# The spectral unit's residual: products with a flipping matrix, or an add on VectorE

## The chip, the cores and the metric

The kernel runs on one core of a Trainium2 chip. The metric is the device time of one execution in microseconds (us). All data is fp32.

## What is computed

The reference is a two-layer block on x of shape (8, 128, 32, 32): 8 images, 128 channels, 1024 tokens each. Every step adds to its own input:

```python
x = x + attention(ln_c(x))          # layer 0, first half
t = to_tokens(x)                    # (8, 1024, 128)
t = t + spectral(ln_t(t))           # layer 0, second half (the STU)
x = from_tokens(t)
x = x + deformable_conv(ln_c(x))    # layer 1, first half
t = to_tokens(x)
t = t + experts(ln_t(t))            # layer 1, second half: 8 experts, the best 2
```

The change concerns one plus sign: the `t +` ahead of the spectral part. That part is a causal convolution over the tokens with 16 filters at four resolutions, each followed by a 128x128 mixing matrix, and three lagged products.

## The kernel before, in words

**Stages.** Attention for all 8 images comes first and writes its result, with its own residual added, to a DRAM tensor `x1d` of shape (image, 128, 8, 128). Then one long stage does the spectral part of all images and, laid between its products, the second layer of the image before. The second layer of the last image runs alone at the end.

**Token orders.** In `x1d[b]` row p holds 8 groups of 128 channels: group par * 4 + i is token 2 * (128 * i + p) + par, so even tokens stand in the first four groups and odd ones in the last four. The spectral part works on tokens in reversed order: an indirect load on POOL's queue (in `prepare`, L1391) reads the rows of `x1d[b]` from the last to the first into a tile `x1`. The norm's source for images 2 to 7 is this tile; for images 0 and 1 the normalised tokens come from loads of their own, made during attention.

**The spectral loop** (`spectral_and_second_layer`). Its work list is (image, filter), 8 x 16 periods, in program order, written out by hand: each engine takes its instructions in that order. A period has two halves (src 0 and 1, the even and odd source tokens). In each half `filter_image` makes three PSUM banks, named p_x, p_y and p_z (L1488). ScalarE turns p_x out twice (L1499, L1500), POOL adds the two (L1501), VectorE takes p_y (L1506, L1509) and p_z (L1516) out with further adds. The sums `us` are mixed one or two periods later: `mix` (L1453, through `add`) multiplies them with the mixing matrices `mf` and accumulates in `po`, a pair of PSUM banks with one buffer for the whole image. The filters of three periods ahead are loaded on SP (L1257, L1258; three buffers, so that the load waits for the products of the present period), and the matrices two periods ahead (L1357; for the first image they are made on VectorE, L1379 and L1381).

**The residual in it.** Ahead of the first mixing product of an image, `start_sums` multiplies each of the 8 groups of `x1` (as weights) with `flip`, the 128x128 matrix with ones on the other diagonal. The product is a turned and re-reversed group, so `po` begins with the residual, in (channel, token) layout, and all other products add to it. The first matmul in each of the two banks carries the start flag (`add` keeps the list `opened`). After the last filter, `finish` copies `po` to `x2` (channels by tokens), one half by ScalarE (L1529) and the other by VectorE (L1530).

**The second layer.** `points` starts with `turn_back`: four TensorE transposes for each half of `x2` into a bank p_back (L1168), and a ScalarE copy of each bank (L1169) to `tok` (128 tokens by 8 groups by channels; group a, row q is token 128 * a + q). Then come the norm of `tok` on VectorE (statistics at L788 and L789), its turn (p_turn, L919), products, the writing of a table to DRAM, and the sampling positions. `sampled` gathers rows of that table (POOL's queue), weighs and sums them on ScalarE and VectorE, takes a norm, and runs the experts (p_e, L1123; L1135, L1140, L1143 on VectorE). Both are generators. `advance` runs them a step at a time in the slots between the spectral products, by a time budget: RATE 3.2 us a slot, and each step says how much it takes. Right after `finish` the new `second_layer(b)` is put at the head of its row, so that `turn_back` is issued in that slot. Apart from `po`, all of the spectral stage's and second layer's PSUM tiles come from one pool of six banks, taken in turn. After the last image, `layer.image` and what is left of the image before alternate, a step each.

Of the kernel before, what the change touches and what calls it, by code (L numbers as in the profile page):

```python
# [11 lines left out]
F32 = mybir.dt.float32  # L12
I32 = mybir.dt.int32
AF = mybir.ActivationFunctionType
ALU = mybir.AluOpType
# [3 lines left out]
P = 128  # L19
B = 8  # L20
C = 128
T = 1024
NT = T // P
HT = T // 2
# [3 lines left out]
NF = 16  # L28
# [774 lines left out]
class DeformAndExperts:  # L803
# [2 lines left out]
    ROWS = T + 33  # L806

    def __init__(
        self, ctx, tc, ident, dram, conv_w, conv_b, off_w, off_b, mask_w, mask_b,
        router_w, router_b, expert_w, expert_b, out, banks,  # L810
    ):
        self.nc = tc.nc
        self.cp = ctx.enter_context(tc.tile_pool(name="d_const", bufs=1))
        self.sb = ctx.enter_context(tc.tile_pool(name="d_sb", bufs=2))
        self.ps = ctx.enter_context(tc.tile_pool(name="d_ps", bufs=banks, space=PSUM))
        self.ident, self.dram, self.out = ident, dram, out
        self.given = (
            conv_w, conv_b, off_w, off_b, mask_w, mask_b, router_w, router_b, expert_w, expert_b
        )
# [162 lines left out]
        got.extend((idx, w))  # L982
        yield

    def image(self, b, x2):

        got = []
        yield from self.points(b, x2, got, True)
        yield from self.sampled(b, got, True)

    def points(self, b, x2, got, alone):


        nc, sb = self.nc, self.sb
        newton = nc.vector if alone else nc.gpsimd
        tok = sb.tile([P, NT, C], F32, tag="tok", name="tok")
        yield from self.turn_back(x2, tok)
        yield
        ht = sb.tile([P, NT, C], F32, tag="ht", name="ht")
        yield from norm_steps(nc, sb, tok, ht, 1e-6, newton, not alone)  # L1000
        yield 1.0 if alone else 5.0
        hc = sb.tile([C, T], F32, tag="hc", name="hc")
        yield from self.turn_steps(ht, hc)
        nc.gpsimd.tensor_tensor(tok, tok, self.cb.unsqueeze(1).to_broadcast([P, NT, C]), ALU.add)
        yield


        tab = self.tabs[b % 2]
        N = TAPS * C + TAPS * 9
        gs = sb.tile([P, NT, N], F32, tag="gs", name="gs", bufs=1)  # L1010
        writes = []

        def write():
            if writes:
                i0, tap, slot, back = writes.pop(0)
                r0 = 33 - back + i0 * P
                queue = nc.scalar if alone and slot % 2 else nc.sync
                queue.dma_start(
                    tab[tap, r0 : r0 + 4 * P, slot, :].rearrange("(i p) c -> p i c", p=P),
                    gs[:, i0 : i0 + 4, tap * C : (tap + 1) * C],  # L1020
                )

        for i in range(NT):
            pg = self.bank("p_g")
            nc.tensor.matmul(
                pg[:, 0:N], hc[:, i * P : (i + 1) * P], self.gw, start=True, stop=True
            )
            nc.scalar.copy(gs[:, i, :], pg[:, 0:N])
            if i % 4 == 3:
                writes += [  # L1030
                    (i - 3, tap, slot, back)
                    for tap in range(TAPS) for slot, back in enumerate((0, 1, 32, 33))
                ]
            for _ in range(4 if alone else 2):
                write()
            yield 1.0 if alone else 1.5
        while writes:
            for _ in range(4 if alone else 2):
                write()
            yield 1.0 if alone else 1.7  # L1040
        po = self.bank("p_om")
        for tap in range(TAPS):
            at = TAPS * C + 9 * tap
            nc.tensor.matmul(
                po[:, 0 : 9 * NT], self.shift[tap], gs[:, :, at : at + 9],
                start=(tap == 0), stop=(tap == TAPS - 1),
            )
        om = sb.tile([P, NT, 9], F32, tag="om", name="om")
        nc.vector.tensor_tensor(
            om, po[:, 0 : 9 * NT].rearrange("p (i k) -> p i k", k=9), self.base, ALU.add  # L1050
        )
        yield
        yield from self.corners(om, got)
        got.append(tok)
# [104 lines left out]
                yield  # L1159
        nc.sync.dma_start(self.out[b].rearrange("c h w -> c (h w)"), ot)  # L1160

    def turn_back(self, src, dst):

        for half in range(2):
            pt = self.bank("p_back")
            for i in range(4):
                t0 = (half * 4 + i) * P
                self.nc.tensor.transpose(pt[:, i * P : (i + 1) * P], src[:, t0 : t0 + P], self.ident)  # L1168
            self.nc.scalar.copy(  # L1169
                dst[:, half * 4 : half * 4 + 4, :].rearrange("p a c -> p (a c)"), pt  # L1170
            )
            yield

    def gates(self, tt, got, wait):
# [122 lines left out]
class Spectral:  # L1297
# [88 lines left out]
    def prepare(self, b):  # L1386

        nc, sb = self.nc, self.sb
        img = {"b": b, "ur": self.given.ur[b % 2], "gap": self.given.given.gap[b % 2]}
        img["x1"] = sb.tile([P, NT, C], F32, tag="x1", name="x1", bufs=2)  # L1390
        nc.gpsimd.indirect_dma_start(  # L1391
            out=img["x1"].rearrange("p i c -> p (i c)"), out_offset=None,
            in_=self.x1d.rearrange("b p i c -> (b p) (i c)"),
            in_offset=bass.IndirectOffsetOnAxis(ap=self.back[:, b : b + 1], axis=0),
        )

        img["ut"] = sb.tile([C, 3, HT + 1], F32, tag="ut", name="ut")
        return img
# [30 lines left out]

    def start_sums(self, img):  # L1430

        po = img["po"] = self.op.tile([P, 2, 2, HT // 2], F32, tag="o", name="po")
        img["opened"] = set()
        for par in range(2):
            for i in range(4):
                out = po[:, i // 2, par, (i % 2) * P : (i % 2 + 1) * P]
                self.add(img, i // 2, out, img["x1"][:, par * 4 + i, :], self.flip)

    def add_lags(self, img):

# [92 lines left out]
def spectral_and_second_layer(tc, spec, layer, weights):  # L1533
    work = [(b, k) for b in range(B) for k in range(NF)]
    imgs = {0: spec.prepare(0)}
# [10 lines left out]
    rows = [deque([spec.channels(imgs[0], layer.bank), layer.setup()]), deque()]  # L1546
    starts = {}
    todo = [0.0, 0.0]

    def second_layer(b):  # L1550
        got = []
        yield from layer.points(b, imgs[b]["x2"], got, False)
        rows[1].append(layer.sampled(b, got, False))

    def advance(time):
# [34 lines left out]
    for n in range(len(work) + 2):  # L1590
        now = work[n] if n < len(work) else None
        if now is not None:
            b, k = now
            if k == 1 and b + 1 < B:
                starts[b + 1] = spec.begin(b + 1, layer.bank, imgs)
                rows[0].append(starts[b + 1])
            elif k == 0 and b:
                for _ in starts[b]:
                    pass
            us = sums[n] = spec.sb.tile([C, 2, 2, HT], F32, tag="us", name="us", bufs=3)  # L1600
        for src in range(2):
            run = iter(())
            if now is not None:
                run = spec.filter_image(imgs[b], src, filters[n], less[n], us, layer.bank)
            for slot, spans in enumerate((SPANS[0:3], SPANS[3:4])):
                next(run, None)
                m = n - 2 + src
                if 0 <= m < len(work):
                    img, k = imgs[work[m][0]], work[m][1]
                    if src == 1 and slot == 0 and k == 0:  # L1610
                        spec.start_sums(img)
                    if src == 1 and slot == 0 and k == 1:
                        spec.add_lags(img)
                    spec.mix(img, 1 - src, spans, mf[m], sums[m], k == NF - 1)
                    if src == 0 and slot == 1 and k == NF - 1:
                        spec.finish(img)
                        if img["b"] + 1 < B:
                            rows[0].appendleft(second_layer(img["b"]))
                if now is not None:
                    advance(RATE if b + 1 < B else LAST_RATE)  # L1620
            next(run, None)
            if now is not None:
                between(n, src)
        if n + 3 < len(work):
            filters[n + 3] = spec.load_filter(work[n + 3][1])
        if NF <= n + 2 < len(work):
            mf[n + 2] = spec.read_matrices(work[n + 2][1])

    runs = [layer.image(B - 1, imgs[B - 1]["x2"]), chain(*rows[0], *rows[1])]
    while runs:  # L1630
        runs = [r for r in runs if next(r, r) is not r]

# [2 lines left out]
def metaformer_kernel(  # L1635
# [30 lines left out]
    with branch.Else():  # L1666
# [4 lines left out]

    spec = Spectral(ctx, tc, dram, phi_e, phi_o, M_u, M_plus, M_minus, coef, x1d, back, begin)
    layer = DeformAndExperts(
        ctx, tc, ident, dram, conv_w, conv_b, off_w, off_b, mask_w, mask_b,
        router_w, router_b, expert_w, expert_b, out, 6,
    )
    with tc.manual_schedule(engines=None):
# [51 lines left out]
```

## Time and profile before

| what | value |
|---|---|
| median of 3 runs | 2700.72 us (2695.61 to 2702.18) |
| the profiled execution | 2699.79 us |
| its span, first to last instruction | 2698.0 us |
| mean granted TensorE clock | 0.974 |
| busy: TensorE matmul | 2530.0 us, 94% of the span |
| busy: TensorE weight load (overlaps the matmuls) | 1769.3 us, 66% |
| busy: VectorE | 1852.9 us, 69% |
| busy: ScalarE | 1083.5 us, 40% |
| busy: GpSimd (POOL) | 1448.6 us, 54% |
| moved by DMA | 267.10 MB, 99 GB/s over the span |

Attention takes the first 910 us or so, the spectral stage with the second layer of images 0 to 6 runs to about 2560 us, and the last image's second layer to the end. The names in the profile leave buffer numbers out: `x1`, `x2` and `x3` all read `x`, so `po<-flip,x` is the product of `start_sums`, `x<-po` the copies of `finish`, and `p_back<-ident,x` the transposes of `turn_back`. PE is TensorE's matmul, PEld its weight load, DVE VectorE, ACT ScalarE, SPq the queue of SP. An fp32 product appears as two weight loads and two matmuls.

### The profile page before, as it was taken

What the parts mean: (1) busy time and instruction counts of PE and PEld (TensorE: products, weight loads), DVE (VectorE), ACT (ScalarE), POOL (GpSimd) and SP (SyncE); (2) the same over time, 40 slices, a digit from 0 to 9 for tenths busy, and PEclk for the clock granted to TensorE, in tenths of its full rate; (3) what the DMA queues carried; (4) which work ended last, traced back from release to release, by engine and by line L of the source; (5) the groups of instructions that cost most, each with busy time, mean ns of one, the idle gap of its engine ahead of it and who ended that gap; (6) DMA issues with size and microseconds to landing.
All of it is one profiled execution on the core that took longest, in us unless ns stands there. A gap on an engine that the chain in (4) does not pass through costs nothing. (4 is left out here: it accounts for less than half of the span.)

```text
span 2698.0 us, 47432 instructions
## 1 busy us (share of the span) xinstructions
PE 2530.0 (94%) x18896; PEld 1769.3 (66%) x18896; DVE 1852.9 (69%) x2728; ACT 1083.5 (40%) x2030; POOL 1448.6 (54%) x1535
## 2 busy tenths in 40 slices
PE   6999999999999799999999999999999999999924
PEld 3555555555555578777787787778778778777712
DVE  3888888888888455448648649648648657658646
ACT  4666766667667111123223224224214224224232
POOL 4777777777788455446246237237236227226230
PEclk9999999999999899999999999999999999999956
DMA  1000000000000254375275266265266266256151
GB/s 29 2 17 2 17 17 2 17 9 10 9 17 17 83 162 153 119 207 160 73 212 169 71 198 184 71 191 176 79 181 194 71 173 194 79 149 202 40 168 35
DMA packets 204675, 267.10 MB, mean 99 GB/s; under 512 B 20308, under 2 KB 138260, under 8 KB 204448
## 3 DMA queue, kind: packets, MB, share of 16 engines
q1 hardware_dynamic: 181312, 205.27, 26.1%
q0 software_dynamic: 16800, 55.59, 6.2%
q10 hardware_dynamic: 6336, 3.15, 0.4%
q8 instruction: 151, 2.47, 0.4%
q14 instruction: 76, 0.62, 0.1%
HBM read 196.02 MB, written 67.92 MB: 98 GB/s over the span
## 5 line engine op out<-in xcount | busy, mean ns | idle before, releaser
L623 POOL TENSOR_TENSOR t<-e 128x1024 f32<-128x1024 f32 x256 | 608.3, 2376 | 199.3 <-ACT e L614 199.0
L651 DVE TENSOR_TENSOR e<-e,rb 128x2048 f32<-128x2048 f32 x256 | 570.8, 2278 | 84.1 <-PE rb L644 84.1
L614 ACT ACTIVATE e<-s 128x2048 f32<-128x2048 f32 x256 | 481.2, 1880 | 253.2 <-PE s L609 250.7
L1501 POOL TENSOR_TENSOR part<-us,part 128x256 f32<-128x256 f32 x256 | 189.9, 743 | 708.5 <-ACT part L1500 707.8
L1453 PE MATMUL po<-us,mf 128*128 128x128 f32 (+2 forms) x2048 | 528.9, 381 | 5.9 <-DVE mf L1381 3.8
L1506 DVE TENSOR_TENSOR part<-p_y,part 128x512 f32<-128x512 f32 x256 | 175.4, 685 | 310.0 <-PE p_y L1488 193.2
L1499 ACT COPY us<-p_x 128x256 f32<-128x256 f32 x256 | 94.8, 370 | 723.2 <-PE p_x L1488 712.8
L1453 PEld LDWEIGHTS po<-us,mf 128*128 128x128 f32 x2048 | 308.2, 191 | 37.5 <-issue 4.8
L609 PE MATMUL s<-q,k 32*128 32x256 f32 x4096 | 296.1, 403 | 14.5 <-ACT e L614 13.7
L661 PE MATMUL av<-e,vt 128*32 128x256 f32 x4096 | 287.9, 388 | 5.3 <-DVE e L651 4.0
L1516 DVE TENSOR_TENSOR us<-p_z,part 128x512 f32<-128x512 f32 x256 | 174.8, 683 | 151.7 <-PE p_z L1488 151.3
L1488 PEld LDWEIGHTS p_z<-diff,gap 128*128 128x128 f32 x1024 | 193.1, 191 | 129.6 <-issue 88.3
L609 PEld LDWEIGHTS s<-q,k 32*128 32x128 f32 x4096 | 186.4, 185 | 137.5 <-ACT e L614 116.3
L1488 PE MATMUL p_z<-diff,gap 128*128 128x256 f32 x1024 | 266.1, 382 | 3.6 <-DVE base L906 3.1
L1095 ACT ACTIVATE g<-g,w 128x128 f32<-128x128 f32 x512 | 161.2, 393 | 118.1 <-DMA g<-tab,here 91.1
L1077 POOL DMA_INDIRECT g<-tab,here x168 | 167.3, 996 | 71.8 <-issue 31.6
L661 PEld LDWEIGHTS av<-e,vt 128*32 128x32 f32 x4096 | 101.3, 109 | 142.2 <-issue 84.3
L1103 DVE TENSOR_REDUCE x<-g 128x128 f32<-128x1536 f32 x64 | 180.4, 2819 | 7.5 <-ACT g L1095 1.5
L1239 POOL TENSOR_TENSOR diff<-teto 128x516 f32<-128x516 f32 x127 | 163.6, 1288 | 1.6 <-DMA teto<-in_phi_o 0.8
L637 DVE RECIPROCAL r<-z 128x256 f32<-128x256 f32 x64 | 112.5, 1757 | 69.5 <-PE z L630 69.3
L1488 PE MATMUL p_y<-diff,gap 128*128 128x256 f32 x512 | 152.6, 379 | 0.1
L1488 PE MATMUL p_z<-teto,ht 128*128 128x256 f32 x512 | 132.3, 381 | 0.0
(264 smaller groups left out, 3731.9 us busy)
## 6 DMA issues: line engine op xcount, KB each, us to landing
mf<-mfd SPq DMA_DIRECT2D x112, 512.0 KB
tab<-gs SPq DMA_DIRECT2D x180, 256.0 KB
teto<-in_phi_o SPq DMA_DIRECT2D x127, 256.5 KB
teto<-in_phi_e SPq DMA_DIRECT2D x127, 256.0 KB
mfd<-mf SPq DMA_DIRECT2D x16, 512.0 KB
xc<-in_x SPq DMA_DIRECT2D x8, 512.0 KB
x1d<-xt SPq DMA_DIRECT2D x8, 512.0 KB
m_room<-in_M_plus SPq DMA_DIRECT2D x16, 256.0 KB
```

The lines of the kernel that those rows point to most:

```text
L609: nc.tensor.matmul(s[:, j, c, :], img["k"][rows, hg, 2 * r + c, :], q[rows, qc * QU : (qc + 1) * QU], start=True, stop=True,)
L614: nc.scalar.activation(e.rearrange("p j c q -> p (j c q)"), s.rearrange("p j c q -> p (j c q)"), AF.Exp, scale=float(HD) ** -0.5,)
L623: nc.gpsimd.tensor_add(t, e[:, :, 0, :], e[:, :, 1, :])
L651: nc.vector.tensor_tensor(e, e, un["rb"].unsqueeze(2).to_broadcast([P, NH, 2, QU]), ALU.mult)
L661: nc.tensor.matmul(qrt["av"][32 * j : 32 * j + 32, 0:QU], img["v"][:, 2 * r + c, P * hg + 32 * j : P * hg + 32 * j + 32], un["e", r][:, j, ...
L1077: nc.gpsimd.indirect_dma_start(out=tiles[-1][:, tap].rearrange("p k c -> p (k c)"), out_offset=None, in_=rows, in_offset=bass.IndirectOffs ...
L1103: nc.vector.tensor_reduce(x3[:, i, :], g.rearrange("p t k c -> p c (t k)"), AX.X, ALU.add)
L1453: self.nc.tensor.matmul(out, lhsT, rhs, start=bank not in img["opened"], stop=last, skip_group_check=True)
L1488: nc.tensor.matmul(out, weights, moving, start=start, stop=stop, skip_group_check=True)
L1501: nc.gpsimd.tensor_add(part[:, 0], mine[:, :, 0:P], part[:, 1])
L1506: nc.vector.tensor_tensor(part[:, 2:4], y[:, 0].unsqueeze(1).to_broadcast([C, 2, 2, P]), part[:, 0:2], ALU.add)
L1516: nc.vector.tensor_tensor(result(2, 4), z, part[:, 2:4], ALU.add)
```

## The change

`start_sums` no longer multiplies; the first mixing product of each bank carries the start flag. The residual is added where `x2`, turned back into tokens, leaves PSUM: `turn_back` takes one more operand and uses VectorE's add in place of ScalarE's copy. That operand, `x1n`, is the same rows of `x1d`, loaded in natural token order: four DMAs an image on SP, two halves by two parities, each 64 rows of 4 x 128 values to every second partition. They are issued in the period after that of the image's filter 13 (the third last). `x1n` has one buffer in the second layer's pool; `x1` goes from two buffers to one. The norm of the spectral part still reads `x1`, and the indirect load is still made for every image. `x1d` is handed to the second layer's class, and `x1n` through `second_layer`, `image` and `points` to `turn_back`.

```diff
-    def points(self, b, x2, got, alone):
+    def residual(self, b):
+
+        x1 = self.sb.tile([P, NT, C], F32, tag="x1n", name="x1n", bufs=1)
+        got = x1.rearrange("q (i two) c -> q two i c", two=2)
+        for half in range(2):
+            src = self.x1d[b, 64 * half : 64 * half + 64].rearrange(
+                "p (par i) c -> p par i c", par=2
+            )
+            for par in range(2):
+                self.nc.sync.dma_start(got[par:P:2, half], src[:, par])
+        return x1
+
+    def points(self, b, x2, got, alone, x1):
...
-        yield from self.turn_back(x2, tok)
+        yield from self.turn_back(x2, tok, x1)
...
-    def turn_back(self, src, dst):
+    def turn_back(self, src, dst, more):
...
                 self.nc.tensor.transpose(pt[:, i * P : (i + 1) * P], src[:, t0 : t0 + P], self.ident)
-            self.nc.scalar.copy(
-                dst[:, half * 4 : half * 4 + 4, :].rearrange("p a c -> p (a c)"), pt
-            )
+            part = [t[:, half * 4 : half * 4 + 4, :].rearrange("p a c -> p (a c)") for t in (dst, more)]
+            self.nc.vector.tensor_tensor(part[0], pt, part[1], ALU.add)
             yield
...
-        img["x1"] = sb.tile([P, NT, C], F32, tag="x1", name="x1", bufs=2)
+        img["x1"] = sb.tile([P, NT, C], F32, tag="x1", name="x1")
...
-        po = img["po"] = self.op.tile([P, 2, 2, HT // 2], F32, tag="o", name="po")
+        img["po"] = self.op.tile([P, 2, 2, HT // 2], F32, tag="o", name="po")
         img["opened"] = set()
-        for par in range(2):
-            for i in range(4):
-                out = po[:, i // 2, par, (i % 2) * P : (i % 2 + 1) * P]
-                self.add(img, i // 2, out, img["x1"][:, par * 4 + i, :], self.flip)
...
                     if src == 1 and slot == 0 and k == 0:
                         spec.start_sums(img)
+                    if src == 1 and slot == 0 and k == NF - 3:
+                        img["tokens"] = layer.residual(img["b"])
...
-                            rows[0].appendleft(second_layer(img["b"]))
+                            rows[0].appendleft(second_layer(img["b"], img["tokens"]))
...
-    runs = [layer.image(B - 1, imgs[B - 1]["x2"]), chain(*rows[0], *rows[1])]
+    last = imgs[B - 1]
+    runs = [layer.image(B - 1, last["x2"], last["tokens"]), chain(*rows[0], *rows[1])]
```

More of the change, by code (lines that the diff above doesn't have):

```diff
@@ L808, in __init__ @@
     def __init__(
-        self, ctx, tc, ident, dram, conv_w, conv_b, off_w, off_b, mask_w, mask_b,
+        self, ctx, tc, ident, dram, x1d, conv_w, conv_b, off_w, off_b, mask_w, mask_b,
         router_w, router_b, expert_w, expert_b, out, banks,
@@ L815, in __init__ @@
         self.ps = ctx.enter_context(tc.tile_pool(name="d_ps", bufs=banks, space=PSUM))
-        self.ident, self.dram, self.out = ident, dram, out
+        self.ident, self.dram, self.out, self.x1d = ident, dram, out, x1d
         self.given = (
@@ L983, in corners, with image @@
         yield
-    def image(self, b, x2):
+    def image(self, b, x2, x1):
         got = []
-        yield from self.points(b, x2, got, True)
+        yield from self.points(b, x2, got, True, x1)
         yield from self.sampled(b, got, True)
-    def points(self, b, x2, got, alone):
+    def residual(self, b):
[9 more added lines that the diff above has]
+    def points(self, b, x2, got, alone, x1):
         nc, sb = self.nc, self.sb
@@ L1548, in spectral_and_second_layer, with second_layer @@
     todo = [0.0, 0.0]
-    def second_layer(b):
+    def second_layer(b, x1):
         got = []
-        yield from layer.points(b, imgs[b]["x2"], got, False)
+        yield from layer.points(b, imgs[b]["x2"], got, False, x1)
         rows[1].append(layer.sampled(b, got, False))
@@ L1673, in metaformer_kernel @@
     layer = DeformAndExperts(
-        ctx, tc, ident, dram, conv_w, conv_b, off_w, off_b, mask_w, mask_b,
+        ctx, tc, ident, dram, x1d, conv_w, conv_b, off_w, off_b, mask_w, mask_b,
         router_w, router_b, expert_w, expert_b, out, 6,
```

## The prediction

> **What bounds the kernel now.** I read the per-core line first (one core, granted clock 0.974), then the busy time by stage, then the rows of the tile that the change touches, then the order of time around one image boundary, the first image and the end.
>
> By stage: columns are the stretch, its length, busy time with instruction counts of PE, PEld, DVE, ACT and POOL, the granted clock, the DMA share, GB/s.
>
> ```profile
> core 0: us, PE busy (x) PEld busy (x) DVE busy (x) ACT busy (x) POOL busy (x), PEclk, DMA share, GB/s
> 1200.00:1400.00 200.00, 196.97 (x916) 153.83 (x915) 136.65 (x265) 57.98 (x181) 87.46 (x119) 1.00 0.50 146
> 1400.00:1600.00 200.00, 197.58 (x922) 154.71 (x921) 133.81 (x255) 60.69 (x188) 88.42 (x129) 1.00 0.49 145
> 2600.00:2650.00 50.00, 0.00 (x0) 0.00 (x0) 35.49 (x61) 20.18 (x64) 23.88 (x25) 0.50 0.51 152
> ```
>
> From about 930 to 2560 us (the spectral stage, with the second layer's work laid between its products) TensorE is busy 98.5 to 99% of each stretch at full clock; VectorE stands at about 67%, ScalarE at 30%. So in this stage a TensorE instruction less is time less, unless a wait behind it grows. The last 138 us are another regime, where TensorE is idle and the last image's serial chain sets the end.
>
> ```profile
> L1453 PEld LDWEIGHTS po<-flip,x x128: 190/192/192, 928.0 to 2364.5; 128*128 128x128 f32 x128
> L1453 PE MATMUL po<-flip,x x128: 272/275/275, 928.2 to 2364.6; 128*128 128x128 f32 x128
> ```
>
> These are the removed products: 8 calls an image, each as two instructions in fp32, 16 weight loads and 16 matmuls an image, 8 images. The 272 to 275 ns are latencies that overlap; the price has to come from spacing in order of time (start, duration, instruction, idle time before it):
>
> ```profile
> 1113.31 0.85 PEld L1453 LDWEIGHTS po<-us,mf 128*128 128x128 f32 x6
> ...
> 1114.19 0.41 PEld L1488 LDWEIGHTS p_y<-teto,ht 128*128 128x128 f32 x2
> ...
> 1117.69 1.32 ACT L1169 COPY tok<-p_back 128x512 f32<-128x512 f32 x2 [0.74 <-PE p_back L1168]
> ...
> 1119.74 0.84 PEld L1488 LDWEIGHTS p_x<-teto,ht 128*128 128x128 f32 x4
> ...
> 1120.15 0.69 DVE L1516 TENSOR_TENSOR us<-p_z,part 128x512 f32<-128x512 f32 x1 [2.48 <-PE p_z L1488]
> 1120.60 1.97 PEld L1453 LDWEIGHTS po<-flip,x 128*128 128x128 f32 x16
> ```
>
> In the same view the next loads start at 1122.49 (po<-us,mf) and 1123.26 (p_y). The flip products have no idle time before or behind them. VectorE stood still 2.48 us up to 1120.15, just when ScalarE turned out the two p_back banks.
>
> The first image is different:
>
> ```profile
> 927.95 1.97 PEld L1453 LDWEIGHTS po<-flip,x 128*128 128x128 f32 x16
> ...
> 933.91 1.35 PEld L1453 LDWEIGHTS po<-us,mf 128*128 128x128 f32 x6 [3.99 <-DVE mf L1381]
> ```
>
> There TensorE runs out of flip products and then stands 3.99 us until VectorE has made the first mixing matrix.
>
> The end, VectorE's queue:
>
> ```profile
> 2560.25 0.69 DVE L1530 COPY x<-po 128x512 f32<-128x512 f32 x1 [4.34 <-ACT x L1529]
> ...
> 2561.83 0.69 DVE L1135 TENSOR_TENSOR ge<-p_e,gates 128x512 f32<-128x512 f32 x1 [0.89 <-PE p_e L1123]
> ...
> 2567.62 0.28 DVE L788 BATCH_NORM_STATS2 st<-tok 128x6 f32<-128x128 f32 x1
> ```
>
> From 2561.83 on VectorE works without a pause to the norm of the last image's tokens.
>
> [...]the trace has 1.89 us for 16 pairs, 118 ns each[...]weight loads and matmuls of these pairs overlap, so a pair costs its spacing, not the sum of its two records (192 + 275 ns). [...]the trace's 128x512 fp32 adds from PSUM take 683 to 685 ns.[...]
>
> **The change, part by part.**
>
> *Flip products leave start_sums.* Read by spacing, image 1: from the first flip load at 1120.60 to p_y's load at 1123.26 is 2.66 us, holding 16 flip pairs and 6 mixing pairs. The same 6 mixing pairs directly behind p_x, half a period earlier, take 1114.19 − 1113.31 = 0.88 us. So the removal is worth 2.66 − 0.88 = 1.78 us, not 1.89 (the mixing loads get 0.11 longer when nothing ran ahead for them). Images 2, 3 and 7 show the same 2.66 (1322.45 to 1325.11, 1529.17 to 1531.83, 2362.72 to 2365.38). Seven images: 7 × 1.78 = 12.5 us saved. Ends: 7 × 1.89 = 13.2 above, about half below, see the first rival.
> Image 0: nothing, since the mixing products wait for mf until 933.91 either way; the wait grows from 3.99 to about 5.8 us. Bound: 0 to 1.8 us saved. I take 0.
>
> *turn_back: two ScalarE copies become two VectorE adds.* An image loses 2 × 586 ns on ScalarE and gains 2 × 685 = 1.37 us on VectorE (price from L1135, the same shape, PSUM with an SBUF operand). For the seven boundaries inside the stage: x2's copy ends on VectorE at 1117.67, the transposes are in at 1117.7 and about 1118.4, so the adds fill 1117.7 to 1119.1, inside the 2.48 us pause before 1120.15. At the boundary ahead of image 3 the copy ends at 1524.52 and VectorE's next work starts at 1526.13, a pause of 1.61 us for 1.37. The waiting instruction is the add; queued behind it on VectorE are the expert products' add (L1135), then the z turn-out (L1516); neither holds TensorE within 5 us, because the z sums are used half a period later[...]. Cost 0; without that cover up to 1.37 us an image, 9.6 us. The readers of tok (the norm's statistics) follow on VectorE itself, so they do not start later. A gain is left out: no wait of TensorE in the trace names ScalarE's tok copies.
> TensorE's wait for x2 at each boundary (1.53 us, then 0.31) stays: it ends with the copies of finish, which are not changed.
>
> *The last image's turn_back.* The first add fits the 0.89 us pause before 2561.83. The second comes in program order behind one expert group, in the unbroken stretch, and pushes the norm, and all that follows in the serial end, by 0.69 us. Bounds 0 and 1.37; I take +0.7.
>
> *The residual's loads.* Four DMAs an image on SP, 128 KB each in rows of 512 bytes, 1024 packets in all. SP issues one in about 0.43 us (its row for the filter loads): 1.7 us an image. They are placed in the period with k = 14 and follow on SP the filter and matrix loads that end at 1475.2 for image 2; the next filter load waits for TensorE until 1489.37, so the 1.7 us lie in idle SP time. In the trace 512-byte packets take 27 ns at the median: 1024 × 27 / 16 = 1.7 us per DMA engine, where the DMA share is 0.28 (1475 to 1500). Needed at 1524: 49 us of lead. Cost 0; bounds 0 and 1.7 us an image, were transfers the limit.
>
> *x1 with one buffer instead of two.* POOL's indirect load (L1391, 0.97 us, at 1312.83 for image 3) now waits for the last reader of the image before: with the flip products gone, the norm of image 2, over 150 us earlier. Cost 0. The loads for images 0 and 1, now read by nobody, remain.
>
> Sum: −12.5 + 0 + 0.7 = −11.8 us. The profiled execution took 2699.79 us (span 2698.0), and becomes 2688.0. The median of the three runs is 2700.72, 0.9 above, so the same step from it gives 2688.9; I take 2688.0.
>
> **Rivals.**
> *A: the time turns into other waits.* In the same stage TensorE already waits on VectorE elsewhere:
>
> ```profile
> PEld p_turn L919 <- DVE tt L795: 11.8, 16, 1.2
> ```
>
> With 10.1 us more on the matmul's own side, some 22 us in all, about 3 us an image near 1476, where VectorE is busy 44 of 50 us. If VectorE's chain there doesn't move up with TensorE, up to the whole 1.78 us is lost again. Against it: between 1350 and 1375 VectorE is busy 6.4 of 25 us, so it has no backlog to carry from the boundary to 1476; it would start earlier as TensorE does. If three quarters are lost: 2699.8 − 3.1 + 0.7 = 2697.4, no change.
> *B: slower, the residual lands late.* The add then stands at the head of VectorE's queue with the z turn-outs behind it; TensorE runs on for about 5 us (half a period to the mixing of those sums) and then stands as well. It decides from 49 + 5 us between issue and landing. At 58 us: 8 × 4 − 11.8 = +20, 2720. For it: the loads stand in SP's single queue behind 1 MB of other loads; against it: the DMA share of 0.28 there.
> *C: more than the sum.* Image 0 gives its 1.8, the last add hides and spacing gives 1.89: 2699.8 − 15.0 = 2684.8.
>
> **From cases to numbers.** Forecast 0.70, A 0.20, B 0.05, C 0.05. About 0.3%, 8 us, is what a measurement of this kernel can tell from no change. Forecast and C lie beyond it: faster 0.75, same 0.20, slower 0.05. The range goes from C less about 2 us for the spread of medians (the three runs lie from 2695.61 to 2702.18) to A: 2683 to 2697; the forecast's own runs from 2684 to 2692.
>
> **What would show it.** Right: no po<-flip,x rows; po<-us,mf directly behind p_x with a p_y load 0.88 us later at each boundary; the wait for mf in image 0 near 5.8 us; p_back read by two adds of about 0.69 us with no idle time on a DMA; stretches of the stage at 98.5% as before. The stage should end near 2547.5 instead of 2560, and the remainder be 0.7 us longer. Wrong: p_turn's waits above 30 us (A), an add with a DMA named before it (B), or a second-layer step that comes late enough that TensorE's share falls below 98%.

## The result, and the profile after

| | before | after |
|---|---|---|
| median of the runs | 2700.72 us | 2685.70 us (2682.64 to 2687.66, 5 runs) |
| ratio | | 0.9946, interval 0.9930 to 0.9962 |
| the profiled execution | 2699.79 us | 2682.64 us |
| first and last finish copy (ScalarE's `x<-po`), end of span | 1116.32, 2559.61, 2698.0 us | 1115.45, 2541.78, 2680.9 us |

The change takes 15.0 us off the median. The interval allows 10 to 19 us; the forecast was 11.8 us and a time of 2688.0, within 2683 to 2697. The execution that was profiled is the fastest of the five: its last finish copy lies 17.8 us earlier than in the profile before, where the forecast had 12.5, so the two profiles show more of a gain than the medians do.

By stage, in the columns of the view before (stretch, length, busy time of PE, PEld, DVE, ACT and POOL, granted clock, DMA share, GB/s):

```profile
1200.00:1400.00 200.00, 197.89 (x917) 155.06 (x917) 135.34 (x264) 57.83 (x182) 88.41 (x129) 1.00 0.50 153
1400.00:1600.00 200.00, 197.59 (x914) 154.51 (x914) 138.38 (x267) 59.45 (x187) 88.31 (x119) 1.00 0.50 150
```

TensorE is as busy as before, 98.8 to 98.9%: what was taken out wasn't replaced by idle time. VectorE's share is hardly changed.

The boundary ahead of image 1, in order of time. Before, 16 weight loads with the flipping matrix stood between p_x and the mixing products:

```profile
1116.83 1.42 DVE L1182 TENSOR_TENSOR tok<-p_back,x1n 128x512 f32<-128x512 f32 x2
...
1118.87 0.84 PEld L1495 LDWEIGHTS p_x<-teto,ht 128*128 128x128 f32 x4
...
1119.28 0.69 DVE L1523 TENSOR_TENSOR us<-p_z,part 128x512 f32<-128x512 f32 x1 [1.04 <-PE p_z L1495]
1119.73 0.85 PEld L1460 LDWEIGHTS po<-us,mf 128*128 128x128 f32 x6
...
1120.61 0.41 PEld L1495 LDWEIGHTS p_y<-teto,ht 128*128 128x128 f32 x2
```

The mixing loads follow p_x at once, and p_y's load 0.88 us later, as the forecast's working had it. The two adds start with the transposes, fill 1.42 us of VectorE's pause (2.48 us before, 1.04 now) and wait for no DMA.

The row of the adds, with the least, the median and the longest duration in ns:

```profile
L1182 DVE TENSOR_TENSOR tok<-p_back,x1n x16: 681/692/693, 1116.8 to 2546.9; 128x512 f32<-128x512 f32 x16
```

An add takes 692 ns; the forecast used 685 from the same shape at another line.

The first image (TensorE's weight loads):

```profile
928.54 0.84 PEld L1495 LDWEIGHTS p_x<-teto,xc 128*128 128x128 f32 x4
934.17 1.14 PEld L1460 LDWEIGHTS po<-us,mf 128*128 128x128 f32 x5 [4.79 <-DVE mf L1392]
```

The first mixing product starts at 934.17 us, at 933.91 before: image 0 saves nothing there, since the product starts when VectorE has made the matrix, with or without the flip products.

The end, VectorE's queue:

```profile
2543.14 0.69 DVE L1182 TENSOR_TENSOR tok<-p_back,x1n 128x512 f32<-128x512 f32 x1
2544.00 0.69 DVE L1147 TENSOR_TENSOR ge<-p_e,gates 128x512 f32<-128x512 f32 x1 [0.17 <-PE p_e L1135]
...
2546.90 0.68 DVE L1182 TENSOR_TENSOR tok<-p_back,x1n 128x512 f32<-128x512 f32 x1
2547.50 0.68 DVE L1147 TENSOR_TENSOR ge<-p_e,gates 128x512 f32<-128x512 f32 x1
...
2550.40 0.28 DVE L788 BATCH_NORM_STATS2 st<-tok 128x6 f32<-128x128 f32 x1
```

The first add lies in a pause that is now 0.17 us, the second in the unbroken stretch. From the finish copy on ScalarE to the first statistics of the norm are 8.62 us (2541.78 to 2550.40), 8.01 before (2559.61 to 2567.62). To the end are 139.1 us, 138.4 before.

The loads, in SP's queue, for image 2:

```profile
1469.34 3.19 SPq L1000 DMA_DIRECT2D x1n<-x1d  x4
1483.21 0.33 SPq L1268 DMA_DIRECT2D teto<-in_phi_e  x1
```

They take SP 3.2 us here and 2.6 us for images 1 and 3, 0.6 to 1.2 us each, not the 1.7 for four of the forecast, and lie where it said, ahead of 10 us in which SP waits for the next free filter buffer.

### The profile page after: what moved, and what is told of

It reads as the page before. It is cut to its first block, busy times and chain, and to the rows that moved or that the text cites. A ratio compares the mean times of both kernels' runs of the same rounds, so it can differ in the third digit from the quotient of the medians.

```text
span 2680.9 us, 47231 instructions
## 1 busy us (share of the span) xinstructions
PE 2518.2 (94%) x18768; PEld 1758.2 (66%) x18768; DVE 1857.6 (69%) x2744; ACT 1074.7 (40%) x2014; POOL 1448.4 (54%) x1535
## 5 line engine op out<-in xcount | busy, mean ns | idle before, releaser
L609 PE MATMUL s<-q,k 32*128 32x256 f32 x4096 | 296.9, 404 | 14.3 <-ACT e L614 13.5
```

Source lines behind the costliest of these rows:

```text
L609: nc.tensor.matmul(s[:, j, c, :], img["k"][rows, hg, 2 * r + c, :], q[rows, qc * QU : (qc + 1) * QU], start=True, stop=True,)
```

## The experiments

After the result two things had to be tested: that each term of the sum has its size alone, and where the gain beyond 12.5 us came from, if it is real. **Theory L**: the products are worth 12.5 us wherever they stand, and the rest is spread between executions. **Theory C**: the rest comes from TensorE's clock. The trace keeps a record of the granted clock, and between 1000 us and the last finish copy it has stretches of 3.41 us at half clock, three in the profile before and three in the one after, with 1.5 to 2.3 us of stalls on the matmul's side in the 3.41 us ahead of each; a kernel with other stalls, or with stalls at other times, has other such stretches. Rivals to both: adds and loads cost or bring something of their own. Ratios are to the kernel before, in runs taken beside those of the experiment on the same chip. Times of different sets of runs are compared by these ratios.

**The products taken out, nothing put in.**

```diff
-            part = [t[:, half * 4 : half * 4 + 4, :].rearrange("p a c -> p (a c)") for t in (dst, more)]
-            self.nc.vector.tensor_tensor(part[0], pt, part[1], ALU.add)
+            self.nc.scalar.copy(
+                dst[:, half * 4 : half * 4 + 4, :].rearrange("p a c -> p (a c)"), pt
+            )
...
-                        img["tokens"] = layer.residual(img["b"])
+                        img["tokens"] = None
```

> The products are gone and nothing takes their place: no loads of x1n, no add, the two ScalarE copies of p_back as before (the residual is left out of the result). The sum's theory: 12.5 us less than the kernel before, 0.7 more of a gain than its forecast of 11.8 for the whole change, so about 2688 and a ratio of 0.9954; the last finish copy lies 138.4 us before the end as in the kernel before. Rival: the add and the loads cost something hidden in the stage; then this kernel is faster than the whole change by several us (below 2682). Rival: part of the change's 15.0 us comes from the copies that left ScalarE; then this kernel gains clearly less than 12.5 us.

Measured: 2686.20 us, ratio 0.9940 (0.9924 to 0.9955). It is neither faster by several us nor clearly slower than the whole change: the whole gain is in the products; the add and the loads cost at most what the intervals leave, a few us, and the copies that left ScalarE bring nothing that shows. The gain of 16 us lies above 12.5, whose ratio would be 0.9954, just inside the interval.

**The products put back into the changed kernel.**

```diff
+        po = img["po"]
+        for par in range(2):
+            for i in range(4):
+                out = po[:, i // 2, par, (i % 2) * P : (i % 2 + 1) * P]
+                self.add(img, i // 2, out, img["ur"][:, par * 4 + i, :], self.flip)
```

> The changed kernel with eight products an image put back at their old place, loads and adds staying (the products take the normalised tokens as weights, so the residual part of the result is wrong; their number and shape are the old ones). The sum's theory: the changed kernel plus 7 x 1.78 = 12.5 us, which is 0.7 us above the kernel before, ratio 1.000 (0.998 to 1.002). Rival, that adds and loads cost in the stage: up to 9.6 us above the kernel before, ratio 1.0036. Rival, that they bring something by themselves: below the kernel before by 3 us, ratio 0.999, with shorter waits of TensorE on p_turn and us.

Measured: 2703.23 us over 14 runs, ratio 0.9999 (0.9990 to 1.0008). Adds and loads beside the old products cost 0 within 0.1%, where the bounds of the forecast reached to 9.6 us; 0.7 is inside. Putting the products back costs 14 us by the ratios on the changed kernel (0.9946) and 16 on the kernel without products (0.9940); 12.5 is inside the intervals of both steps.

**The products issued twice in the kernel before.**

```diff
         for par in range(2):
             for i in range(4):
                 out = po[:, i // 2, par, (i % 2) * P : (i % 2 + 1) * P]
                 self.add(img, i // 2, out, img["x1"][:, par * 4 + i, :], self.flip)
+        for par in range(2):
+            for i in range(4):
+                out = po[:, i // 2, par, (i % 2) * P : (i % 2 + 1) * P]
+                self.add(img, i // 2, out, img["x1"][:, par * 4 + i, :], self.flip)
```

> The kernel before with the eight products of each image issued twice (the residual counts twice). The sum's theory: the second set costs 1.89 us (its spacing, 16 pairs of 118 ns) in seven images and nothing in image 0, where the wait for the first mixing matrix falls from 3.99 to about 2.1 us: +13.2 us, 2714, ratio 1.0049. Rival, image 0 is not free: +15.1. Rival, TensorE's time is given back in waits: well under 13, with the waits p_turn <- tt shorter by what is missing.

Measured: 2713.12 us, ratio 1.0032 (1.0022 to 1.0042), 8.6 us by the ratio. A miss: 13.2 lies outside. And the p_turn waits are not the place, they are about as long as before (1.5 to 1.8 us an image, 2.3 in the last). So one set of eight products was worth 16 us and the next one 9, together about what the spacing gives for two (12.5 + 13.2). Theory L doesn't hold as it stands.

The mean granted clock is on record for each run of these sets, to 0.001. One less this mean, times the span, is an estimate of the time that TensorE lost to the lower clock:

| kernel | runs | mean time | mean granted clock | lost to the clock |
|---|---|---|---|---|
| no products | 6 | 2687.3 us | 0.9738 | 70.3 us |
| before | 27 | 2703.3 us | 0.9734 | 71.7 us |
| products twice | 14 | 2712.4 us | 0.9751 | 67.6 us |

Most of the loss, some 50 us in the profile before (138.4 us at a granted clock of 0.63), lies behind the last finish copy, where TensorE is busy for 45.2 us. But the kernel with the products twice lost 4.1 us less than the kernel before, and the standard errors of the two means are 1.0 and 0.6. With the loss taken out, in a reckoning that counts each microsecond of it in full, the steps are 14.6 and 13.3 us in place of 16.0 and 9.1. So the small second step is mostly the clock's, as theory C has it. The first is not: it stands 2 us above 12.5 with a standard error of 1.2. Why the kernel with the products twice lost less stays open.

**The loads late.**

```diff
-                    if src == 1 and slot == 0 and k == NF - 3:
-                        img["tokens"] = layer.residual(img["b"])
...
                     if src == 0 and slot == 1 and k == NF - 1:
+                        img["tokens"] = layer.residual(img["b"])
                         spec.finish(img)
```

> The changed kernel with the four loads issued in the slot of finish instead of three filters earlier. SP reaches them right after the filter and matrix loads of that period, about 6 us ahead of the first add instead of 49, behind some 1 MB of other transfers. At 160 GB/s these take 6.5 us and the residual's 0.5 MB 3 more, so the first add starts 4 to 5 us late. The sum's theory of its second rival: VectorE stands for that time and TensorE, which has about 5 us before it needs the next us, loses 0 to 2 us an image: 0 to +14 us on the changed kernel (2686 to 2700), and the add's idle time names a DMA. If TensorE had no such slack, 8 x 4.5 = +36 us.

Measured: 2685.74 us, ratio 0.9936 (0.9922 to 0.9950): no loss. The forecast's 160 GB/s is the rate of the profile before from 1310 to 1320 us. VectorE's adds in order of time, with their idle time:

```profile
1117.87 1.29 DVE L1182 TENSOR_TENSOR tok<-p_back,x1n 128x512 f32<-128x512 f32 x2 [5.62 <-DMA x1n<-x1d]
1313.60 1.29 DVE L1182 TENSOR_TENSOR tok<-p_back,x1n 128x512 f32<-128x512 f32 x2 [2.82 <-DMA x1n<-x1d]
```

The wait that the forecast's slower rival was built on is now real: VectorE stands 1.6 to 5.6 us at the head of seven boundaries, 21 us in all, for a DMA. And TensorE pays nothing for it that shows. In the first of them p_y and p_z of that half follow one another on TensorE as in the changed kernel, while VectorE is 5.6 us late. So the five microseconds of tolerance that the forecast claimed are there, at this one boundary; at the others VectorE is at most 3 us late. A longer delay, from which that rival would start to cost, was not tried.

**Four adds in place of one.**

```diff
-            self.nc.vector.tensor_tensor(part[0], pt, part[1], ALU.add)
+            for _ in range(4):
+                self.nc.vector.tensor_tensor(part[0], pt, part[1], ALU.add)
```

> The changed kernel with every add of turn_back issued four times (same operands, same result): 4.1 us more on VectorE at each boundary. The sum's theory, that TensorE doesn't wait for VectorE within 5 us of a boundary: nothing in the stage, and the last image's serial end longer by six adds, 4.1 us: 2690. Rival, the adds had just fitted their pause and anything over it is paid: 7 x (5.5 - 1.6 to 2.5) + 4.1 = 25 to 31 us, 2711 to 2717.

Measured: 2691.55 us over 22 runs, ratio 0.9971 (0.9962 to 0.9980). The changed kernel beside it had 2686.83: +4.7 us for 4.1 expected, and 25 to 31 are out. In this kernel's profile the last finish copy on ScalarE starts at 2543.76, and the norm of the last image at:

```profile
2556.42 0.28 DVE L788 BATCH_NORM_STATS2 st<-tok 128x6 f32<-128x128 f32 x1
```

That is 12.66 us, 8.62 in the changed kernel and 8.01 before: the two adds cost 0.6 us there, and six more 4.0. The cost of an add is in the serial end, and the stage takes three more of them free.

**The changed kernel again.**

> The changed kernel as it is, once more, as the base of the three beside it and to see whether its gain is nearer to the sum's 11.8 us or to the 16 that the run without products and the run with late loads showed. Linear theory (eight products are worth 12.5 us wherever they stand): ratio 0.9956. Theory of stalls and clock: products are worth their 1.78 us an image, and the rest is that fewer of TensorE's stalls (on p_turn, us and p_back) are followed by a 3.4 us stretch at half clock, each worth some 1.7 to 2.5 us: ratio 0.994, and the profile of this run shows three or so such stretches between 1000 and 2560 us, each right after a stall of 2 us and more.

Measured: 2686.83 us, ratio 0.9946 (0.9927 to 0.9966), the same as the first time; 0.9956 and 0.994 are both inside, so it doesn't decide between the theories. Its clock record has five half-clock stretches between 1000 and 2545 us. One of them, with TensorE's weight loads around it, and then the busy times of the 3.41 us ahead of it and of the stretch itself (PE first, PEld second, the granted clock third from the end):

```profile
1263.74 0.14 PEld L919 LDWEIGHTS p_turn<-ident,tt 128*128 128x128 f32 x1 [0.76 <-issue]
1264.37 0.14 PEld L919 LDWEIGHTS p_turn<-ident,tt 128*128 128x128 f32 x1 [0.49 <-DVE tt L795]
1265.55 0.44 PEld L919 LDWEIGHTS p_turn<-ident,tt 128*128 128x128 f32 x2 [1.05 <-DVE tt L795]
1265.88 1.39 PEld L1495 LDWEIGHTS p_z<-diff,gap 128*128 128x128 f32 x4
1267.37 1.58 PEld L1495 LDWEIGHTS p_z<-teto,ht 128*128 128x128 f32 x4
1268.98 0.84 PEld L1495 LDWEIGHTS p_x<-teto,ht 128*128 128x128 f32 x4
```

```profile
1262.05:1265.46 3.41, 1.79 (x8) 0.78 (x6) 3.41 (x7) 0.59 (x1) 2.18 (x3) 1.00 1.02 323
1265.46:1268.87 3.41, 3.31 (x9) 2.70 (x10) 1.82 (x5) 0.59 (x1) 0.00 (x0) 0.50 0.23 68
```

TensorE waits in pieces for VectorE's norm, 1.6 us in all on the matmul's side: in the 3.41 us ahead of the stretch that side was busy for 1.79. The eight z loads behind the waits take 2.97 us, where 1.68, twice the 0.84 of the four p_x loads behind the stretch, is their time at full clock. The five stretches last 3.413 us each, and start at 1265.46, 1678.47, 2091.48, 2344.07 and 2490.84: 121, 121, 74 and 43 times 3.413 us apart.

In this execution, among images 2 to 6, those with one stretch took 207.27 and 207.81 us from finish copy to finish copy, those without 204.87 to 205.66. So an image with a stretch is about 2 us longer; some 0.5 us of it is that its waits are longer too (the matmul's side idle for 2.79 and 3.06 us, in the others for 2.11 to 2.55).

**p_turn later.**

```diff
         yield from norm_steps(nc, sb, x3, tt, 1e-5, newton, not alone)
-        yield 1.0 if alone else 5.0
+        yield 1.0 if alone else 9.0
```

> The changed kernel with four more us of budget between the second norm of an image and its turn (p_turn<-ident,tt), so that other work stands on TensorE while VectorE and POOL finish the norm. In the changed kernel's profile these waits add up to 19.5 us in seven images. Theory of stalls and clock: they shrink to a few us, and of the stretches at half clock those behind p_turn go: 12 to 25 us less than the changed kernel. Rival A of the prediction, VectorE's chain bounds that place: the waits stay where they are in sum (on p_turn, or on us behind it), and the time too.

Measured: 2676.28 us, ratio 0.9917 (0.9897 to 0.9936), 8 to 11 us less than the changed kernel beside it, where 12 to 25 were expected; run once more, with the next three:

> The changed kernel with the later p_turn once more, as the base without half-clock stretches for the three beside it: 0.990 to 0.992 of the kernel before, no half-clock stretch between 1000 and 2540 us.

2674.11 us, ratio 0.9898 (0.9883 to 0.9913). Both profiles have no half-clock stretch in the stage after image 0. But the stall didn't vanish. The waits of TensorE's matmul side (us in total, times, the longest), in the changed kernel's second profile, then in this kernel's second:

```profile
PE p_turn L919 <- DVE tt L795: 11.4, 19, 1.0
```

```profile
PE p_gt L1226 <- DVE gates L1220: 10.9, 6, 1.8
```

11.4 us in 19 pieces on one tile became 10.9 us in 6 on the next one of the same chain: for that wait rival A was right, VectorE's chain bounds it and only its place moves. Yet no stretch follows now. The 3.41 us around one of the six waits, in this kernel's second profile, and the 3.41 us behind:

```profile
1280.21:1283.62 3.41, 1.57 (x7) 1.02 (x7) 2.20 (x7) 0.59 (x3) 0.65 (x1) 1.00 0.00 0
1283.62:1287.03 3.41, 3.41 (x14) 2.24 (x13) 2.08 (x4) 0.81 (x4) 0.00 (x0) 1.00 0.00 0
```

The matmul's side is busy for 1.57 us here, less than the 1.79 that a stretch followed above. So the length of the wait alone, as the profile has it, doesn't tell whether a stretch follows; one wait or several pieces may be the difference, but no run tests that.

How much of the gain is the clock's isn't settled. By the granted clock of all runs the loss is 69.8 us in the changed kernel (7 runs) and 68.2 in this one beside it (6 runs), 1.6 us of a gain of 8 to 11, with a standard error of 2.6. In the second set it is 62.8 us, 8.5 less than in the kernel before beside it, of a gain of 27.5 us over that kernel by medians, of which the change alone brings 14 to 15.

**The products in a kernel without stretches.** The kernel with the later p_turn, with the products put back as in the second experiment, once and twice:

> The later p_turn, with the eight products of each image put back (normalised tokens as weights, so the residual part of the result is wrong). Where no stall is followed by a half-clock stretch, the products should cost what spacing says: 7 x 1.78 = 12.5 us on the kernel beside it, 0.0046 in the ratio. If they cost 16 us here too, the price of a product is larger than its spacing and the clock isn't the reason.

> As the kernel with the products kept, with each of them issued twice. Clock theory: a second set costs 7 x 1.89 = 13.2 us more than the first, so the two steps are about equal (12.5 and 13.2), where with the stalls in place they were 16 and 9. Rival: the steps stay unequal, and the difference has nothing to do with the stalls.

| kernel | median | ratio, interval | first to last finish copy |
|---|---|---|---|
| no products | 2674.11 | 0.9898 (0.9883 to 0.9913) | 1418.84 us |
| products once | 2687.61 | 0.9952 (0.9938 to 0.9965) | 1430.56 us |
| products twice | 2699.28 | 0.9996 (0.9987 to 1.0004) | 1443.09 us |

The steps are 13.5 and 11.7 us by the medians, 14.6 and 11.9 by the ratios; the runs alone don't part 12.5 from 16. The last column is from the busy time of that one stretch in each profile; none of the three has a half-clock stretch in it:

```profile
1112.21:2531.05 1418.84, 1398.58 (x6463) 1095.50 (x6463) 972.39 (x1855) 414.31 (x1306) 634.02 (x906) 1.00 0.50 151
```

```profile
1113.69:2544.25 1430.56, 1410.76 (x6575) 1107.78 (x6575) 974.02 (x1855) 414.80 (x1305) 634.32 (x906) 1.00 0.50 149
```

```profile
1112.67:2555.76 1443.09, 1423.43 (x6687) 1120.56 (x6687) 973.29 (x1855) 414.49 (x1305) 634.25 (x906) 1.00 0.50 148
```

112 instructions more (7 images by 16) are 11.72 us more, and 112 again 12.53: 1.67 and 1.79 us an image, beside 1.78 and 1.89 of the working. Here the price of a product is its spacing, and the second costs what the first did. With the stalls in place the steps were 16 and 9. That the two differ there and not here fits theory C, and so does the clock on record: these three kernels lost the same to it, 62.8, 61.8 and 62.9 us by the mean of their runs, where those with the stalls differed by 4. The single profiles don't show it: with stalls they have three to five stretches (before 3, changed 3 and 5, kept 4, twice 5) without a clear order, and the one of the products twice is the slowest of its 14 runs.

**turn_back a slot later.** The forecast had let TensorE's wait for x2 at each boundary stay. It can be covered:

```diff
     def second_layer(b, x1):
         got = []
+        yield RATE
         yield from layer.points(b, imgs[b]["x2"], got, False, x1)
```

> The changed kernel with turn_back one slot later (the second layer's generator first takes one slot's budget): the z and x products of the next half stand between finish and the transposes. The forecast said that TensorE's waits for x2 (1.53 and 0.31 us a boundary, more at image 6's) stay because finish isn't changed; if they are waits and nothing else, this takes them away in seven images: 12.9 us less than the changed kernel, 2673. If a stretch at half clock goes with one of them, 2 us more. Rival: the wait only moves, to the mixing product that needs po free, and the time is that of the changed kernel.

Measured: 2671.75 us (2669.99 to 2673.46), ratio 0.9897 (0.9876 to 0.9919), 15 us less than the changed kernel beside it by the medians, 13 by the ratios. In order of time at the boundary after image 0:

```profile
1115.43 0.85 PEld L1460 LDWEIGHTS po<-us,mf 128*128 128x128 f32 x6
1116.31 1.01 PEld L1180 LDWEIGHTS p_back<-ident,x 128*128 128x128 f32 x8
1117.29 0.30 PEld L1495 LDWEIGHTS p_y<-teto,ht 128*128 128x128 f32 x2
```

No idle time is left before p_back, nor does po hold up the mixing product there. The size agrees with 12.9, but not the parts: all that follows in the second layer moved by a slot too, the p_turn waits fell (PEld 12.9 us to 3.3), new ones came on p_y for POOL's filter differences (9.5 us), and one stretch at half clock is left where the changed kernel beside it has five.

**Both moved.** The two edits in one kernel.

> The changed kernel with turn_back a slot later and p_turn 4 us of budget later. Additive theory: 13 us from the first and 10 from the second, 2663. But the profile of the kernel with only turn_back moved shows the p_turn waits down from 24 to 4 us and one half-clock stretch, so most of the second's gain is in the first already: 2665 to 2671, 0 to 6 us under that kernel.

Measured: 2672.80 us, ratio 0.9892 (0.9877 to 0.9907), outside the expected 2665 to 2671: nothing is gained on top. With both, TensorE waits at five boundaries for VectorE's copy of po (0.8 us each), and for POOL on p_y as above (9.8 us of its weight loads). The three kernels with a moved step (0.9892 to 0.9917, intervals that overlap) can't be told apart; each beats both the kernel before and the changed one.

## Why the prediction was right, point by point

- **TensorE is the bound of the stage, and the products' price is their spacing.** Right. 1.78 us an image shows in the trace at the boundary, and as 1.67 and 1.79 us in the kernels without stretches. Reading the 272 ns records instead would have given 7 x 16 x 0.27 = 30 us. The mixing products are 2048 matmuls in both profiles, so opening the banks of `po` took no further one.
- **Image 0 gives nothing.** Right at the place named: its first mixing product starts 0.26 us later than before. The wait before it is 4.79 us, not 5.8, because the products ahead of it ran later in that execution.
- **The adds are covered.** Right, and with room: three more of each at every boundary are free in the stage, and a VectorE that stands 5.6 us at one of them doesn't hold up TensorE either.
- **The last add costs 0.7 us.** Right: the last image's norm starts 0.6 us later behind the finish copy, and 4.0 us later still with six more adds. The whole serial end doesn't show it, since it varies more: 138.4 us before and 139.1 after, but 142.0 in another execution of the same kernel.
- **The loads.** Hidden as said. SP's time for them was undersized, 2.6 to 3.2 us for 1.7: its price was taken from the filter loads, and these take longer to issue. It costs nothing because the wait behind them is 10 us.
- **x1 with one buffer.** No wait of POOL names it.
- **Rival A** didn't come: on the matmul's side the p_turn waits add up to 10.1 us before, and to 8.9 and 11.4 in the two profiles after. Its size was misread: the 22 us of the forecast add the waits of the weight loads and of the matmuls, but these are the same waits seen twice (at 1478.8 us in the profile before both stand for the same `tt`). So it is 10 to 12 us, about 1.5 an image and not 3. Only the experiment with the later p_turn showed that this wait is bound by VectorE and goes along with its chain.
- **Rival C** has the number that came, 15.0 us, but not its parts: image 0 gave nothing at the place named, the last add didn't hide, and the boundary gave 1.78 us, not 1.89. The number alone can't tell it from the forecast.
- **What the sum left out.** The measured 15.0 and, a second time, 14.1 us against 11.8 are within the intervals, so nothing more has to be explained. The clock isn't shown to be the rest: in the second set the kernel before and the changed one lost the same to it (70.2 and 69.8 us, granted clock 0.9740 in both), and in the five runs of the result the changed kernel's clock was lower, 0.9724, where the kernel before had 0.9734 to 0.9740 beside the three sets of experiments. What the sum did leave out is that a stall cost more than its length where a stretch at half clock followed: it priced all instructions at full clock. That shows in the uneven steps of one and two sets of products, and moves single executions by about 2 us a stretch.

## What to carry to other kernels

Price a removed matmul by the spacing to its neighbours in order of time, with what comes after it, not by its record (1.78 us an image here, where 16 records of 272 ns are 4.35); and see what was hidden by it (here a wait of 3.99 us in the first image) before counting it for every turn of the loop. An operation moved to a less busy engine can be free: here two adds of 692 ns a boundary were, also with VectorE 5.62 us late at one boundary. Delaying it on purpose measures that room. In this kernel, with TensorE 98.8% busy, the images with a stretch at half clock behind short stalls took about 2 us longer; compare the granted clock of all runs, not of one profile, before a difference is put down to it. Moving the step that stalls can be worth as much as removing work (13 to 15 us here for turn_back a slot later, 15.0 for the change).

## What the runs showed of the hardware that was not expected

- Between 1000 us and the last finish copy the stretches at half clock lasted 3.41 us each (three in the profile before, three and five in the two profiles of the changed kernel), and in each of these executions they started whole multiples of 3.413 us apart. In the 3.41 us ahead of each of the six in the profiles before and after, the matmul's side stood 1.5 to 2.3 us, in a stage where it is 98.8% busy. But in the kernel with the later p_turn it stood 1.8 us in one piece (1.57 of 3.41 us busy), and no stretch followed. Eight loads took 2.97 in place of 1.68 us at such a stretch, and an image with one took about 2 us longer.
- VectorE's add of 128x512 fp32 from PSUM with an SBUF operand took 692 ns; SP took 0.6 to 1.2 us to issue a DMA of 64 partitions with rows of 512 bytes, and 0.33 to 0.43 us for most filter loads of 256 KB.
